# A four-stage transformer block on one core: moving transfers, landing rooms and waits in the second attention

## The chip, the core and the metric

The kernel runs on one core of a Trainium2 chip. The metric is the device time of one launch in microseconds (us). Engines are named as in the profile: PE is TensorE (matmuls), DVE is VectorE, ACT is ScalarE, POOL is GpSimd, and SP is SyncE, which issues most of the DMAs. "SPq" and "POOLq" are the issue queues of SP and POOL.

## The reference, cut to what matters

Four residual steps on `x` of 2 x 1024 rows by 512, all in float32:

```python
x = x + attn_a(layernorm(x))   # gated linear attention: 4 heads, chunks of 128 rows, carried state
x = x + ffn(layernorm(x))      # silu(gate) * up, then down; int32 weight codes, hidden size 1408
x = x + attn_b(layernorm(x))   # below
x = x + ffn(layernorm(x))      # the same weights again

def attn_b(x, W_q, W_k, W_v, W_o):
    Q, K, V = x @ W_q, x @ W_k, x @ W_v           # one head of 512
    attn = softmax(Q @ K.T / sqrt(512), axis=-1)  # 1024 x 1024 for each of 2 batches
    return (attn @ V) @ W_o
```

Most of the change lies in `attn_b`. It is computed with the weights folded beforehand (`wm` holds W_q times W_k transposed, `wvo` holds W_v times W_o), so that a tile of output is the probabilities times V', plus the residual row, divided by the sum of its row.

## The kernel before, in words

Rows are worked in 16 tiles of 128 (`NT` = 16, 8 for each batch). A float32 operand of PE is kept as a high and a low half: `split(hi, lo, src)` is a cast on ACT (`hi`, line 70) and a subtraction on DVE or POOL (`lo`, line 71); `mm3` (lines 84 to 86) multiplies with three matmuls, high by high, high by low and low by high. Each engine runs its instructions in the order in which the scheduler of the kernel's language has put them. `behind(...)` states that what follows is to stand behind given instructions; the lists `last`, `summed`, `ends` and `splits` hold such instructions. A DMA from SP is issued in that order too, and waits ahead of its issue for what it reads and for the room that it fills.

The stages, with their places in the span:

- The start: products of weights (`M` from W_q and W_k, `V` from W_v and W_o) are computed on PE, split and stored to DRAM by `spill` (line 168; two stores a block, high and low half). Layer norm of the first eight tiles goes through `ln_tile`, which ends in `layernorm`: statistics on DVE, the power -1/2 on POOL (`rs`, line 109), the scaling on DVE (`xn`, line 111), then a transpose on PE (`pxT`, line 119).
- Attention a: a loop over 16 tiles; `fill[t]` holds steps to be slipped in behind tile t. `a_split(2)` and `a_split(3)`, the splits of the normed rows of tiles 8 to 11 and 12 to 15, are in `fill[2]` and `fill[6]`. `kT` (line 601) is the copy of a tile's keys, needed by the scores `pS` (line 627).
- ffn f: two passes, with seven products where the block form has eight (`pX`, `pY`, `pZ`, `pV`, line 329). `stationary` (line 302) makes or loads the weights of one of 11 blocks; the first time, it casts int32 codes on ACT (`codes`) and keeps the result in DRAM (`wc`). Later passes load 896 KB for each block (`wcf`, `wcg`).
- Attention b: two batches b, each with four cycles n = 0 to 3. A cycle is written out as `scores_head` (four PSUM tiles, `psX`, `psV`, `psY`, `psZ`), something in between (`q_proj` or an `out_b`), `scores_tail`, and `softmax` of the tiles 2n and 2n+1: maxima `mx` and scaling `nm` on DVE, exponentials `pe` on ACT, row sums, `ri`.
- ffn g: like ffn f, from stored weights.

A tile's probabilities are turned so that PE can use them. `probs_T` transposes 32x32 blocks on DVE (`py`, line 1059), stores them to DRAM (`p<-py`, line 1063, 512 KB), and reads them back in four DMAs that place each block (`raw<-p`, line 1072, 128 KB each, in pieces of 32 floats). `raw` lands in a buffer with the tag `pe`, the room of the exponentials, of which there are two. `probs_split` casts it to `pth` and subtracts to `ptl`; `out_b` multiplies these with V' (24 matmuls into `pob`, lines 84 to 86) and adds the residual row `xrb`, loaded on POOL, on DVE (line 1097); line 1098 stores the result. Tile 14 is turned on PE (`ppt`) instead.

Between these steps the layer norm of ffn g goes on for the tiles that are done (`norm`: `ln_norm` for a tile, `ln_move` for a group of four tiles). `ln_move` turns a group by 16 small DMAs from SBUF to SBUF (`xT_g<-y_g`, line 199, 64 KB each, again in pieces of 32 floats). `moving` holds the steps of `combine`, which make ffn g's operands (`B_g`, `T_g`) from a turned group. `do(steps, n)` runs the next n of such a list behind the last softmax. The order of these calls is written out by hand in the loop over b that is printed below.

Of the kernel before, what the change touches and what calls it, by code (L numbers as in the profile page):

```python
# [16 lines left out]
P = 128  # L17
# [17 lines left out]
def hybrid_block_kernel(ctx: ExitStack, tc: tile.TileContext, a, out):  # L35
# [132 lines left out]
    def spill(pool, tags, ps, dst, name):  # L168
        for m in range(KD):
            hi, lo = (pool.tile([P, 512], F32R, tag=tags[m % len(tags)], name=f"{name}{m}_{j}") for j in range(2))  # L170
            done = split(hi, lo, ps[m])
            nc.sync.dma_start(out=dst[m][:, 0:512], in_=hi.bitcast(F32))
            nc.sync.dma_start(out=dst[m][:, 512:1024], in_=lo.bitcast(F32))
        return done

    lnT, lnY, lnX = {}, {}, {}
# [13 lines left out]
    def ln_move(nm, st, b):  # L190

        if b == 0:
            lnT[nm, st] = slot(f"xT_{nm}{st}").rearrange("p (k c) -> p k c", k=KD)
        y = lnY[nm, st]
        xf = lnT[nm, st].bitcast(F32).rearrange("p k (i b q) -> p (k i) b q", i=ST, b=4)
        for c in range(4):
            half = (nm, st) in (("b", 2), ("g", 0))
            sync = nm in "af" or (nm, st) in (("b", 0), ("b", 1), ("g", 3)) or (half and c % 2)
            (nc.sync if sync else nc.gpsimd).dma_start(
                out=xf[32 * b : 32 * (b + 1), :, c, :],  # L200
                in_=y[32 * c : 32 * (c + 1), b].rearrange("p k i q -> p (k i) q"),
            )
# [96 lines left out]

    saves = []  # L300

    def stationary(j, name, fresh=None, loaded=None, queue=None):


        w = slot(f"wc{name}_{j}").rearrange("p (n c) -> p n c", n=8)
        if fresh or loaded:
            a21, a11, s1, s2, s3, a12, s4, a22 = (w[:, n] for n in range(8))
            for n, (dst, nm) in enumerate(((w[:, 1:6:4], "cg"), (w[:, 0:8:7], "cu"))):
                room = (loaded[n], None) if loaded else fresh
                codes(*room, dst, a["wgu"][j][:, n * 512 : (n + 1) * 512], f"{nm}{name}_{j}")  # L310
            f = lambda x: x.bitcast(F32)
            nc.gpsimd.tensor_tensor(s1, f(a21), f(a22), ALU.add)
            nc.gpsimd.tensor_tensor(s2, f(s1), f(a11), ALU.subtract)
            nc.gpsimd.tensor_tensor(s3, f(a11), f(a21), ALU.subtract)
            nc.gpsimd.tensor_tensor(s4, f(a12), f(s2), ALU.subtract)
            saves.append(lambda: nc.sync.dma_start(out=wc_d[j], in_=f(w[:, 1:8])))
        else:
            (queue or nc.sync).dma_start(out=w[:, 1:8].bitcast(F32), in_=wc_d[j])
        return w

    def products(ps, w, nm, pr, n, first):
# [17 lines left out]
    with ExitStack() as actx:  # L339
# [354 lines left out]
        for i in range(4):  # L694
            ends.clear()
            q_head(0, i)
            with behind((wq_loaded, *ends.values())):
                for t in ((), (4,), (5,), (6, 7))[i]:
                    ln_tile(t)
            if i == 1:  # L700
                with behind((*normed_x, *copied)):
                    spill(ap, ("kT", "kw", "sdec", "at"), pm, m_d, "M")
# [17 lines left out]
                step()  # L720
            xTa[g] = lnT["a", g]

        fill[2].append(lambda: a_split(2))
        fill[6].append(lambda: a_split(3))
        moving = combine("f", 0)
        wcs, loads = [], []
        for t in range(NT):
            if t + 4 < NT:
                q_head(*divmod(t + 4, ST))
            if t == 0:  # L730
                decay_rows(0)
                load_row(0)
                load_row(1)
            load_row(t + 1)
            if t + 1 < NT:
                kv_tile(t + 1)
            weighed = scores(t)
            if t + 1 < NT:
                with behind((*(normed[t + 1][2:] or normed[t][2:]), *key_copy)):
                    decay(t + 1)  # L740
            if t == NT - 2:
                with behind(key_copy):
                    for n in (1, 2):
                        loads.append(product_operands(sp, a["WvT"], a["Wo"], "V", n))
                with behind(parts[-4:]):
                    late_norm.pop()()
            with behind(normed.get(t + 1, (weighed,))):
                for step in fill[t]:
                    step()
                if 1 <= t <= KH:  # L750
                    down_weights(sp, t - 1)
                for n in {NT - 3: (0,), NT - 1: (3,)}.get(t, ()):
                    loads.append(product_operands(sp, a["WvT"], a["Wo"], "V", n))
                if t == NT - 3:
                    first_codes = [
                        load_codes(xp, "xn", a["wgu"][0][:, n * 512 : (n + 1) * 512], f"cf0_{n}") for n in range(2)
                    ]
# [159 lines left out]
    with ExitStack() as bctx:  # L917
# [104 lines left out]
        def softmax(t, halves, casts=()):  # L1022
            mx = mp.tile([P, 2], F32, tag="mx", name=f"mx{t}")
            for s, x in enumerate(halves):
                nc.vector.tensor_reduce(mx[:, s : s + 1], x, AX.X, ALU.max)
            nm = mp.tile([P, 1], F32, tag="nm", name=f"nm{t}")
            nc.vector.tensor_scalar(nm, mx[:, 0:1], mx[:, 1:2], -SC, ALU.max, ALU.mult)
            pe = bp.tile([P, T], F32, tag="pe", name=f"pe{t}")
            rs = mp.tile([P, 2], F32, tag="rsum", name=f"rsum{t}")
            for s, x in enumerate(halves):  # L1030
                with behind(casts):
                    act = nc.scalar.activation(
                        pe[:, s * 512 : (s + 1) * 512], x, AF.Exp, bias=nm, scale=SC, accum_out=rs[:, s : s + 1]
                    )
            ri = mp.tile([P, 1], F32, tag="ri", name=f"ri{t}")
            nc.vector.tensor_tensor(ri, rs[:, 0:1], rs[:, 1:2], ALU.add)
            last[:] = act.ins, nc.vector.reciprocal(ri, ri).ins
            pes[t] = pe, ri

        def probs_T(b, i):  # L1040
# [24 lines left out]
            )  # L1065
            lo = bp.tile([P, NK, P], F32R, tag="ptl", name=f"ptl{t}")
            hi = bp.tile([P, NK, P], F32R, tag="pth", name=f"pth{t}")

            raw = bp.tile([P, T], F32, tag="pe", name=f"raw{t}").rearrange("p (k c) -> p k c", k=NK)
            placed = p_d[i].rearrange("k (c j) (r q) -> r j (k c) q", c=4, r=4)  # L1070
            for r in range(4):
                nc.sync.dma_start(  # L1072
                    out=raw[32 * r : 32 * (r + 1)].rearrange("p k (c q) -> p (k c) q", c=4), in_=placed[r]
                )
            ptT[t] = hi, lo, raw, ri

        def probs_split(b, i, after):
# [11 lines left out]
        def out_b(b, i):  # L1089
            t = b * NK + i  # L1090
            hi, lo, _, ri = ptT[t]
            xr = rp.tile([P, D], F32, tag="xres", name=f"xrb{t}")
            nc.gpsimd.dma_start(out=xr, in_=x2[t])
            po = psum(f"pob{t}")
            for k in range(NK):
                mm3(po, hi[:, k, :], lo[:, k, :], vs[b, k][0], vs[b, k][1], k == 0, k == NK - 1)
# [14 lines left out]
            vs[b, kt] = h_, l_  # L1111

        splits = []
        qs, QA, heads, pes, ptT, vs, last, summed = {}, {}, {}, {}, {}, {}, [], []

        def do(steps, n):
            with behind(last):
# [10 lines left out]
        def cycle(b, n, between):  # L1128

            array(scores_head, b, n)  # L1130
            if n > 0:
                for i in (2 * n - 2, 2 * n - 1):
                    if (b, i) != (1, 5):
                        probs_split(b, i, summed)
            if n in (0, 2):
                with behind(summed):
# [2 lines left out]
            if n == 1:  # L1139
                q_operands(b, 2, False)  # L1140
            array(scores_tail, b, n)
            if n < 3:
                with behind(last):
                    q_operands(b, n + 1, True)
# [3 lines left out]
        for b in range(NB):  # L1148
# [35 lines left out]
            for i in (0, 1):  # L1184
                probs_T(b, i)
            do(norm, 2)

            def between():
                q_proj(b, 1, (2, 3))
                if b:  # L1190
                    with behind(summed):
                        do(norm, 2)

            cycle(b, 1, between)
            for i in (2, 3):
# [100 lines left out]
```

## Time and profile before

| | |
|---|---|
| median of 3 runs | 958.59 us (958.22 to 959.99) |
| the profiled execution | 958.89 us, span 957.2 us |
| PE busy | 934.8 us, 98% of the span |
| DVE, ACT, POOL busy | 721.6, 412.4, 224.2 us |
| granted TensorE clock, mean | 0.995 |
| DMA | 162.18 MB in 218,805 packets, 155,056 of them under 512 bytes |

The span runs from the first to the last instruction of the profiled execution. Engines work side by side, so their busy times do not add up to it. The page of the profile also gives the span in 40 slices, with each engine's busy share and the clock that TensorE was granted, in tenths. Other views list what an engine waited for, the chain of waits that sets an end, and the sums of windows. Numbers at the end of a waits row are the total in us, the count and the longest; a landing time runs from a DMA's issue to its arrival.

The batch loop of attention b covers some 490 to 733 us. In its second batch, PE runs: scores of cycle 0 from 622.3, cycle 1 from 637.5, cycle 2 from 658.2, cycle 3 from 685.0; the last three `out_b` follow `ppt` at 706.

### The profile page before, as it was taken

To read this page: it belongs to the slowest core of one execution; us is meant where nothing else is said; L and a number is where in the kernel's file an instruction comes from. 1 tells how busy PE (TensorE), PEld (TensorE's weight loads), DVE (VectorE), ACT (ScalarE), POOL (GpSimd) and SP (SyncE) were. 2 spreads that over 40 slices of the span, in tenths; PEclk is the share of its full clock that TensorE was granted. 3 is DMA by queue.
4 is the path that set the end of the run, shared out by engine and by line. 5 is a ranking of instruction groups with operands and counts; after the bars stand their busy time and mean duration, and the time that the engine had idled before them with its cause. 6 is when DMAs were issued, how large, how long until landed. Compare 5 with 4: busy or idle time off the path is not lost.

```text
span 957.2 us, 13215 instructions
## 1 busy us (share of the span) xinstructions
PE 934.8 (98%) x4402; PEld 775.2 (81%) x4402; DVE 721.6 (75%) x1461; ACT 412.4 (43%) x795; POOL 224.2 (23%) x324
## 2 busy tenths in 40 slices
PE   9999999999999999999999999999896999999998
PEld 7788888898788878888888888888675888888887
DVE  7767767779899699769938778489675976976655
ACT  5554343345665344345234443244342443534421
POOL 3233323444553011111121302023200341001100
PEclk9999999999999999999999999999998999999999
DMA  9426456675898457724735879157987762463112
GB/s 326 171 100 176 133 122 170 195 184 195 295 331 292 116 189 260 205 45 149 267 69 95 170 154 245 64 97 150 160 173 229 271 190 45 177 239 145 39 60 84
DMA packets 218805, 162.18 MB, mean 169 GB/s; under 512 B 155056, under 2 KB 170736, under 8 KB 218736
## 3 DMA queue, kind: packets, MB, share of 16 engines
q1 hardware_dynamic: 215120, 151.10, 54.8%
q0 software_dynamic: 3616, 10.23, 5.0%
q8 instruction: 35, 0.57, 0.3%
q14 instruction: 34, 0.28, 0.1%
HBM read 104.76 MB, written 41.84 MB: 153 GB/s over the span
## 4 chain that ended last, share of the span: by engine, by line
PE 84%; DVE 5%; DMA 5%; SPq 3%; ACT 2%; issue 1%; POOL 0%; ACTq 0%
PE pog L889 4%; PE pog L888 4%; PE pVg L329 4%; PE pZg L329 4%; PE pXg L329 4%; PE pXf L329 4%; PE pZf L329 4%; PE pVf L329 4%; PE pof L889 3%; PE pof L888 3%; SPq L1072 3%; PE pYg L329 2%; PE pYf L329 2%; DMA raw<-p 2%; PE pob L84 2%; PE pob L85 2%
## 5 line engine op out<-in xcount | busy, mean ns | idle before, releaser
L84 PE MATMUL pob<-vh,pth 128*128 128x512 f32 x128 | 51.6, 403 | 12.0 <-ACT pth L70 12.0
L888 PE MATMUL pog<-wdg,hsg 128*128 128x512 f32 (+1 forms) x165 | 60.1, 375 | 0.0
L889 PE MATMUL pog<-wdg,hsg 128*128 128x512 f32 (+1 forms) x165 | 60.1, 375 | 0.0
L889 PE MATMUL pof<-wdf,hsf 128*128 128x512 f32 x154 | 59.1, 390 | 0.5 <-DVE hsf L71 0.5
L888 PE MATMUL pof<-wdf,hsf 128*128 128x512 f32 x154 | 58.9, 390 | 0.0
L85 PE MATMUL pob<-vl,pth 128*128 128x512 f32 x128 | 51.2, 400 | 0.0
L86 PE MATMUL pob<-vh,ptl 128*128 128x512 f32 x128 | 51.2, 400 | 0.0
L71 POOL TENSOR_TENSOR hsg<-sgg,hsg 128x128 fp32r<-128x128 f32 x40 | 18.0, 470 | 130.6 <-ACT hsg L70 130.6
L329 PE MATMUL pVf<-T_f,wcf 128*128 128x512 f32 x176 | 46.9, 390 | 1.2 <-ACT hbf L816 1.2
L329 PE MATMUL pXg<-B_g,wcg 128*128 128x512 f32 x176 | 46.6, 389 | 0.0
L329 PE MATMUL pVg<-T_g,wcg 128*128 128x512 f32 x176 | 46.3, 389 | 0.0
L329 PE MATMUL pXf<-B_f,wcf 128*128 128x512 f32 x176 | 45.4, 391 | 0.0
L109 POOL TENSOR_TENSOR rs_b<-ve_b,mhalf 128x1 f32<-128x1 f32 x16 | 13.1, 827 | 119.0 <-DVE ve_b L107 118.9
L70 ACT CAST pth<-raw 128x512 fp32r<-128x512 f32 x30 | 17.1, 619 | 55.0 <-DMA raw<-p 55.0
L329 PEld LDWEIGHTS pVf<-T_f,wcf 128*128 128x128 f32 x176 | 33.0, 188 | 8.5 <-ACT hbf L816 1.7
L84 PEld LDWEIGHTS pob<-vh,pth 128*128 128x128 f32 x128 | 24.8, 194 | 18.0 <-ACT pth L70 13.0
L71 DVE TENSOR_TENSOR ptl<-raw,pth 128x512 fp32r<-128x512 f32 x30 | 19.6, 688 | 26.0 <-ACT pth L70 25.9
L329 PEld LDWEIGHTS pXf<-B_f,wcf 128*128 128x128 f32 x176 | 32.9, 188 | 7.2 <-ACT hbf L816 0.4
L329 PEld LDWEIGHTS pXg<-B_g,wcg 128*128 128x128 f32 x176 | 33.0, 188 | 6.9
L329 PEld LDWEIGHTS pVg<-T_g,wcg 128*128 128x128 f32 x176 | 33.0, 188 | 6.9
L888 PEld LDWEIGHTS pog<-wdg,hsg 128*128 128x128 f32 x165 | 31.1, 188 | 5.7
L889 PEld LDWEIGHTS pog<-wdg,hsg 128*128 128x128 f32 x165 | 31.0, 188 | 5.6
(336 smaller groups left out, 2746.8 us busy)
## 6 DMA issues: line engine op xcount, KB each, us to landing
wcg<-wc SPq DMA_DIRECT2D x20, 896.0 KB, 5.3
wc<-wcf SPq DMA_DIRECT2D x11, 896.0 KB, 7.2
wcf<-wc SPq DMA_DIRECT2D x11, 896.0 KB, 5.1
p<-py SPq DMA_DIRECT2D x15, 512.0 KB, 3.8
raw<-p SPq DMA_DIRECT2D x60, 128.0 KB, 4.2
xin_a<-in_x SPq DMA_DIRECT2D x16, 256.0 KB, 5.1
xra<-in_x SPq DMA_DIRECT2D x16, 256.0 KB, 2.8
row<-cl SPq DMA_DIRECT2D x16, 256.0 KB, 3.8
```

Source lines behind the costliest of these rows:

```text
L70: c = nc.scalar.copy(hi, src)
L71: return c.ins, (eng or nc.vector).tensor_tensor(lo, src, hi.bitcast(F32), ALU.subtract).ins
L84: nc.tensor.matmul(ps, lhs_hi, rhs_hi, start=first, stop=False)
L85: nc.tensor.matmul(ps, lhs_hi, rhs_lo, start=False, stop=False)
L86: end = nc.tensor.matmul(ps, lhs_lo, rhs_hi, start=False, stop=last).ins
L109: nc.gpsimd.tensor_tensor(rs, ve, mhalf, ALU.pow)
L329: nc.tensor.matmul(ps, w[:, m, k * P : (k + 1) * P], o[:, s, k, :], start=first and k == 0 and s == 0, stop=k == 1 and s == 1, skip_group_ ...
L888: nc.tensor.matmul(ps, hs[i][0][:, j], wd[j][:, ds], start=j == 0, stop=False)
L889: nc.tensor.matmul(ps, hs[i][1][:, j], wd[j][:, ds], start=False, stop=j == KH - 1)
L1072: nc.sync.dma_start(out=raw[32 * r : 32 * (r + 1)].rearrange("p k (c q) -> p (k c) q", c=4), in_=placed[r])
```

## The change

1. In `probs_T`, `raw` is no longer a buffer of its own: the read lands in the room of the low half `ptl`, and the subtraction of the split works in place. Only tile 15 still uses a `pe` room.
2. In `out_b`, the residual row is loaded by SP, not POOL; for the last three tiles the load stands behind the last read of probabilities. The first two weight blocks of ffn g are loaded by SP too.
3. `ln_move` of group (g, 0) goes wholly on POOL (half of it was on SP). The norm steps of the second batch are given out in other cycles: two steps that stood between the scores of cycle 1 come after the cycle, and two steps of `moving` that stood ahead of cycle 2 come behind the scaling of its last softmax.
4. The split of tile (1, 3) goes behind the scaling `nm` of the last softmax of cycle 2.
5. `spill` stores the low halves of `V` on POOL.
6. `a_split(2)` and `a_split(3)` leave `fill` and go behind the copy of the key at t = 3 and t = 7.
7. `ln_tile` of tiles 5, 6 and 7 goes behind the scaling of the normed tile before (`normed_x`).

```diff
@@ spill
             nc.sync.dma_start(out=dst[m][:, 0:512], in_=hi.bitcast(F32))
-            nc.sync.dma_start(out=dst[m][:, 512:1024], in_=lo.bitcast(F32))
+            low = nc.gpsimd if name == "V" else nc.sync
+            low.dma_start(out=dst[m][:, 512:1024], in_=lo.bitcast(F32))
@@ ln_move
-            half = (nm, st) in (("b", 2), ("g", 0))
-            sync = nm in "af" or (nm, st) in (("b", 0), ("b", 1), ("g", 3)) or (half and c % 2)
+            sync = nm in "af" or (nm, st) in (("b", 0), ("b", 1), ("g", 3)) or ((nm, st) == ("b", 2) and c % 2)
@@ the start
-            with behind((wq_loaded, *ends.values())):
+            with behind((wq_loaded, *ends.values(), *(normed_x if i > 1 else ()))):
                 for t in ((), (4,), (5,), (6, 7))[i]:
                     ln_tile(t)
@@ attention a
-        fill[2].append(lambda: a_split(2))
-        fill[6].append(lambda: a_split(3))
...
+            if t in (3, 7):
+                with behind(key_copy):
+                    a_split(t // 4 + 2)
@@ softmax
-            nc.vector.tensor_scalar(nm, mx[:, 0:1], mx[:, 1:2], -SC, ALU.max, ALU.mult)
+            scaled[:] = [nc.vector.tensor_scalar(nm, mx[:, 0:1], mx[:, 1:2], -SC, ALU.max, ALU.mult).ins]
@@ probs_T
-            raw = bp.tile([P, T], F32, tag="pe", name=f"raw{t}").rearrange("p (k c) -> p k c", k=NK)
+            raw = lo.bitcast(F32)
+            if t == NT - 1:
+                raw = bp.tile([P, T], F32, tag="pe", name=f"raw{t}").rearrange("p (k c) -> p k c", k=NK)
...
-                nc.sync.dma_start(
-                    out=raw[32 * r : 32 * (r + 1)].rearrange("p k (c q) -> p (k c) q", c=4), in_=placed[r]
-                )
+                back[:] = [
+                    nc.sync.dma_start(
+                        out=raw[32 * r : 32 * (r + 1)].rearrange("p k (c q) -> p (k c) q", c=4), in_=placed[r]
+                    ).ins
+                ]
@@ out_b
-            nc.gpsimd.dma_start(out=xr, in_=x2[t])
+            with behind(back if t >= NT - 3 else ()):
+                nc.sync.dma_start(out=xr, in_=x2[t])
@@ cycle
-                    if (b, i) != (1, 5):
+                    if (b, i) not in ((1, 3), (1, 5)):
                         probs_split(b, i, summed)
...
             array(scores_tail, b, n)
+            if (b, n) == (1, 2):
+                probs_split(1, 3, scaled)
+                with behind(scaled):
+                    for _ in range(2):
+                        moving.pop(0)()
@@ the loop over b
-            def between():
-                q_proj(b, 1, (2, 3))
-                if b:
-                    with behind(summed):
-                        do(norm, 2)
-
-            cycle(b, 1, between)
+            cycle(b, 1, lambda: q_proj(b, 1, (2, 3)))
             for i in (2, 3):
                 probs_T(b, i)
-            do(norm, 4)
+            do(norm, 4 if b == 0 else 6)
             array(out_b, b, 0)
             if b:
                 moving = combine("g", 0)
-                do(moving, 2)
...
-        wcs = [stationary(n, "g0", queue=nc.gpsimd) for n in range(2)]
+        wcs = [stationary(n, "g0") for n in range(2)]
```

More of the change, by code (lines that the diff above doesn't have):

```diff
@@ L300, in hybrid_block_kernel, with stationary @@
     saves = []
-    def stationary(j, name, fresh=None, loaded=None, queue=None):
+    def stationary(j, name, fresh=None, loaded=None):
         w = slot(f"wc{name}_{j}").rearrange("p (n c) -> p n c", n=8)
@@ L317, in stationary @@
         else:
-            (queue or nc.sync).dma_start(out=w[:, 1:8].bitcast(F32), in_=wc_d[j])
+            nc.sync.dma_start(out=w[:, 1:8].bitcast(F32), in_=wc_d[j])
         return w
@@ L1113, in hybrid_block_kernel @@
         splits = []
-        qs, QA, heads, pes, ptT, vs, last, summed = {}, {}, {}, {}, {}, {}, [], []
+        qs, QA, heads, pes, ptT, vs, last, summed, back, scaled = {}, {}, {}, {}, {}, {}, [], [], [], []
         def do(steps, n):
```

## The prediction

> **What bounds the kernel now.** I read the page first. TensorE (PE) is busy for 934.8 of 957.2 us, so the kernel is a stream of matmuls and an edit gains only where that stream stands still. The row of clocks has one slice at 8 where the others have 9, and the busy row has an 8 beside it: something is wrong near three quarters of the span.
>
> ```profile
> PE 934.8 (98%) x4402; PEld 775.2 (81%) x4402; DVE 721.6 (75%) x1461; ACT 412.4 (43%) x795; POOL 224.2 (23%) x324
> PE   9999999999999999999999999999896999999998
> PEclk9999999999999999999999999999998999999999
> ```
>
> Then what PE waited for (total, times, longest). The first line is nearly all of it: two waits of `out_b` (PSUM tile pob) for the cast of the probabilities (pth), 12.0 us together.
>
> ```profile
> PE pob L84 <- ACT pth L70: 12.0, 2, 7.8
> PE pxT_a L119 <- DVE xn_a L111: 1.4, 2, 1.0
> PE pVf L329 <- ACT hbf L816: 1.2, 1, 1.2
> PE pS L627 <- ACT kT L601: 1.2, 2, 0.7
> ```
>
> Windows around the two waits (PE busy, DVE, ACT, POOL, clock, DMA share, GB/s) show that each also costs clock afterwards.
>
> ```profile
> 674.60:678.00 3.40, 0.25 (x1) 0.25 (x2) 0.27 (x1) 0.92 (x2) 1.95 (x4) 1.00 1.31 149
> 678.00:681.40 3.40, 3.40 (x9) 2.39 (x9) 3.40 (x8) 1.23 (x4) 0.00 (x0) 0.50 1.42 142
> 722.40:725.80 3.40, 0.00 (x1) 0.01 (x1) 0.02 (x1) 0.67 (x2) 0.00 (x0) 0.50 1.06 255
> 725.80:729.20 3.40, 3.40 (x8) 2.68 (x9) 1.27 (x2) 0.47 (x1) 0.00 (x0) 0.50 0.84 311
> ```
>
> In a half-clock window PE gets through about half (9 and 8 matmuls against 16 or 17 in the windows after), so some 1.75 us is lost each time: by PE's rows the 24 matmuls of out_b(1,2) run from 677.75 to 685.1 and those of out_b(1,7) from 725.8 to 733.1, 7.3 us each, against 5.44 (24 x 0.2267) at full speed. PE's rows leave 4.3 us idle before the first (to 677.75) and 8.0 before the second (to 725.8); 12.0 of these 12.3 is the wait listed. The tail of the second attention so loses 4.3 + 8.0 + 2 x 1.75 = **15.8 us**. That is the cap of any gain there.
>
> Why it waits is in the chain of waits over that stretch (start, us, what).
>
> ```profile
> 665.01 0.32 SPq L1072
> ...
> 677.13 6.49 DMA raw<-p
> 683.72 0.63 ACT pth L70
> ...
> 709.01 1.15 DVE py L1059
> 710.20 3.50 DMA p<-py
> 713.83 0.32 SPq L1072
> 714.20 1.50 SPq L1072
> 715.75 6.13 SPq L1072
> 721.92 3.11 DMA raw<-p
> 725.13 0.63 ACT pth L70
> ```
>
> First stall: the reads `raw<-p` of tiles 10 and 11 are issued from 665.0 to 679.5 and land late. Second: tile 15's exponentials (ACT rows at 707.3 to 708.8) come late, because the cycle before them was late, and then its four reads take 8.65 us to issue beside two 896 KB loads of wcg from POOL. Issue times of eight reads, alone and then in the first stall:
>
> ```profile
> L1072 SPq DMA_DIRECT2D raw<-p x8: 324/828/1826, 643.5 to 649.1; - x8
> DMA to landing us min/median/max: 3.5/4.3/4.6
> L1072 SPq DMA_DIRECT2D raw<-p x8: 318/1948/2562, 665.0 to 677.1; - x8
> DMA to landing us min/median/max: 6.1/7.6/8.7
> ```
>
> **A rule against the change.** What differs at 665 is POOL's 16 moves `xT_g<-y_g` (64 KB each, from 665.2 to 677.3), also in 128-byte pieces. The Trainium skill, "DMA: Bandwidth & Descriptors", section "Why small descriptors are slow (HBM only)", says that transfers between two places in SBUF are spared the penalty of small pieces. By it the moves are no great load, shifting them buys nothing, and the first stall stays (4.3 + 1.75 = 6.05 us less gain). The rows speak otherwise: eight reads are 8,192 pieces (1 MB by 128 bytes) and alone take 9.8 us from first issue to last landing; with the moves' 8,192 beside them it is 18.7 us, the same rate per piece. I follow the rows.
>
> **The change part by part**, on the profiled execution (958.89 us: span 957.2 and 1.69 around it; it stands 0.3 above the median 958.59).
>
> (1) *Reads land in the room of the low half (ptl).* The same 60 reads; no instruction is added. The exponentials' room (pe) comes free at the transpose py, so the next exponentials no longer wait for a cast. In exchange the read of tile t waits for the last matmul of out_b(t-2), and SP's stores and rows stand behind it. On PE about 15 us lie between the end of out_b(t-2) and the start of out_b(t) in batch 1 (669.4 to 685: scores 4.3, out_b 5.4, scores 5.7). First issue to cast takes 6.35 us alone (643.47 to 649.82) and 7.35 with neighbours. The narrowest place is tile 5 of batch 0: out_b(0,3) ends at 563.8, the data is needed at 573.4, so 9.6 us for 7.35: slack 2.
>
> (2) *Norms of g's tiles 6 and 7, and g's moves, come later.* All 16 moves then start behind the read of tile 10, at about 673. Tile 10: read from 665.4 alone, cast about 671.8, needed at 673.5. Tile 11: issued after out_b(1,1), lands about 675.7, needed much later. The first stall and its slow window go; I leave +0.3. Group (g,0)'s moves all go to POOL (8 more at about 0.65 us each, 627 to 638, where POOL is otherwise idle and PE has scores): 0.
>
> (3) *Scaling before splits.* nm of tiles 12 and 13 no longer queues behind the casts of tile 11. With (1), their exponentials come at 678.4 to 681 instead of 686 to 688.6. Downstream, PE itself sets the pace: cycle 3 starts near 680, tile 13's read goes out when out_b(1,3) ends (690.1) and lands at 696.5, casts to 697.9, tile 15's exponentials to 699.3, py 700.7, store 3.7 (landed 704.4), reads 3.7 to issue and 3 to land, cast at 710.8 to 711.2. PE needs it at 711.7 (out_b(1,4) ends 699.9, then two ppt and two out_b). Stall between 0 and 1.2, taken +0.7. The 8.0 and its slow windows go otherwise.
>
> (4) *Rows (16 x 256 KB) and the first wcg go from POOL to SP.* SP waits for the store three tiles back before it issues a row, about 2 us each (its waits of 2.9 and 2.1 us for x<-xrb in that stretch); cover: a row is issued one or two tiles ahead of its use. The last three rows and wcg stand behind tile 15's reads: issued 708 to 709.2. DVE's add for tile 13 then waits until about 712 and holds the second half of tile 15's low part, which out_b(1,7) reaches only 2.7 us after its start: covered. wcg_0 lands 5.3 (median) to 9.3 us (beside the reads) later, at 714.5 to 718.5, needed at 717.2: +0 to +1.3, taken +0.3.
>
> (5) *V's low stores on POOL.* Four stores of 256 KB leave SP, whose next load (codes) starts 2.8 us earlier. The scheduler puts codes of wcf_3 ahead of the cast hbf_0 on ACT, which frees the PSUM that pVf waits for. PE loses 2.4 to 2.85 us at 253 and 259 (pVf 1.2, pYf 0.9). With an earlier load I expect 0.5 to be left: -1.9; bounds -2.5 and +1.5 (hbf_0 behind two code casts of 0.73 us).
>
> (6) *The splits of a's groups 2 and 3 go behind the copy of the key.* ACT no longer does four casts (2.18 us at 88.31) ahead of kT: 1.2 us of waits go, and the first product of the new group waits about 0.45: -0.8.
>
> (7) *The last norms of attention a go behind normed_x.* Tile 4's xn comes earlier, so the wait of 1.0 at 29.4 goes. But rs of tiles 6 and 7 now stands behind two Wv subtractions on POOL (1.3 us each, to 36.4), and their xn behind ten instructions of DVE. Summing DVE's rows, they end at about 39.4 and 40.0; PE needs them from 36.1. pWv starts at 40.6 in place of 38.17: **+2.3**, bounds +1.5 and +2.9.
>
> *The clock there.* The Trainium skill, "TensorE: Matmul & The Clock Gate", "What's actually happening", halves the rate after an idle window of about 3.4 us. The first window above held 0.25 us of work and still brought 0.50. So by the rule a stop of 3.4 us must fill a window exactly and the sum gets +0; by the row a slightly longer reach will do, about one chance in five of +1.75. The likeliest case leaves it out; it is in the range.
>
> Sum: -15.8 + 0.3 + 0.7 + 0.3 - 1.9 - 0.8 + 2.3 = -14.9, so 958.9 becomes **944.0 us**. A difference under 0.2% (1.9 us) could not be told from no change here.
>
> **The rivals.**
> - *A second stall stays (0.14).* Tile 15's store waits on SP behind a row (2 to 3 us each), or its read shares the queues with moves or rows: cast 3 to 5 us late, a slow window, wcg behind it. For it: two of its links (store 3.5, reads 6.13 + 3.11) sit at fixed cost, with only 0.5 us to spare. Against: the wcg loads are now behind it. 944 + 3 to 8 = 947 to 952.
> - *The first stall only moves (0.10).* The move burst meets tile 11's or 13's read instead, or tile 5's: 12.1 us from issue to cast (665.0 to 677.1) against 9.6 is 2.5, and 1.75 of clock, in one or two places: 948 to 952.
> - *Slower (0.12).* SP's in-order queue becomes the bound: a read that waits two tiles back holds the next store, row and x3 store, and DVE's in-order add then stands on the row ahead of the next maxima, so every cycle pays. Place: cycles 2 and 3 of both batches, tile by tile. It decides once a read, from release to cast, takes more than 15 us, some 2 us beyond the collided read plus a row wait (12.1 + 2): six tiles at 1.5 to 2 us with 1.75 of clock each are 19 to 22 us, against 14.9 gained: 963 to 966. Against it: alone, a read takes half that.
> - *It does not do what it says (0.02):* the order of PE's instructions in the second attention is unchanged, and SP's and POOL's lists show each move, so hardly.
>
> **How the numbers follow.** Likeliest case 0.62: 941 to 947. Low end: -15.8 - 2.5 - 1.3 + 1.5 = -18.1, which is 941. The range runs to 953 to take in both middle rivals; outside lie the slower case and a little below. Faster 0.62 + 0.14 + 0.10 = 0.86, same 0.02, slower 0.12.
>
> **What would show it.** The 12.0 of pob for pth gone or under 1.5; all clocks at 9; the eight reads of tiles 10 and 11 near 0.9 us each; pxT_a's wait up from 1.4 to about 3.5; pS for kT gone; the first pXg at 717 to 718 (before 733.0). Wrong, if pob still waits over 3 us, if ppt or psX starts to wait, or if SP stands on pob for over 3 us with a store behind it.

## The result, and the profile after

The changed kernel takes 956.74 us (median of 13 runs, 955.05 to 958.57) where the kernel before takes 958.76 (13 runs, 958.11 to 959.99). The ratio is 0.9979 with a 95% interval of 0.997 to 0.9987: 2.0 us faster, where 14.9 were forecast. The profiled execution of the changed kernel took 955.05 us with a span of 953.3; it is the fastest of the 13, so its span lies 3.9 below that of before while the medians lie 2.0 apart.

From the page (busy time, the 40 slices, the clock) and the view of what PE waited for (total, times, longest):

```profile
PE 936.1 (98%) x4402; PEld 776.3 (81%) x4402; DVE 723.0 (76%) x1461; ACT 412.1 (43%) x795; POOL 220.5 (23%) x318
PE   9899999999899999999999999999999999999998
PEclk9999999999999999999999999999999999999999
...
PE pXf L329 <- ACT u2f L843: 4.7, 1, 4.7
PE pxT_a L119 <- DVE xn_a L111: 3.9, 1, 3.9
PE pob L84 <- ACT pth L70: 2.1, 1, 2.1
```

The 8 near three quarters of the span has gone, and with it 9.9 of the 12.0 us of `pob` for `pth`. Two waits that were not there have come in elsewhere: 4.7 us in ffn f, and 3.9 at the start, where 1.4 stood. The second slice (from 24 us) and the eleventh (from 238 us) now show an 8. Windows around the three stops (length, then busy time of PE, PEld, DVE, ACT and POOL, clock, DMA share, GB/s):

```profile
36.40:39.80 3.40, 0.00 (x0) 0.00 (x0) 3.40 (x10) 1.96 (x4) 2.35 (x3) 0.96 0.83 265
39.90:43.30 3.40, 3.40 (x13) 3.07 (x14) 2.20 (x6) 1.97 (x3) 0.00 (x0) 0.56 0.50 154
257.30:260.70 3.40, 0.00 (x0) 0.00 (x0) 0.00 (x0) 1.65 (x3) 0.13 (x1) 1.00 0.98 338
261.40:264.80 3.40, 3.40 (x10) 2.62 (x9) 1.98 (x4) 0.26 (x2) 2.00 (x3) 0.50 1.03 392
701.60:705.00 3.40, 1.26 (x6) 0.70 (x5) 0.16 (x1) 0.81 (x2) 0.00 (x0) 1.00 1.22 159
705.10:708.50 3.40, 3.40 (x9) 2.39 (x9) 2.48 (x6) 1.18 (x4) 0.00 (x0) 0.50 0.68 116
```

Each stop is followed by a window at half clock, so each costs more than its wait. The mean clock of these two executions hides this (0.995 in both): three half-clock windows were there before (one at 678, two from 722) and three are there after, but at other places. Between executions it shows. The fastest of the 13 of the changed kernel had a mean clock of 0.995, the slowest (958.57 us) 0.991: some two windows more, by the estimate that one takes half of 3.4 us out of 955.

Setting the start of the same PE instruction in one trace against the other gives the account by stage (after minus before): +4.0 us by `pcum` (before at 41.0), back to +2.7 by 143 us after the copies of the key (-1.3), +7.4 in ffn f at 267 us (+4.7), +8.4 when attention b has run to 650 us, and -3.6 at the first `pXg` (729.42, before 732.98). The last step is the tail of attention b: -12.0.

The reads that the change was to spare look as the prediction wanted. For tiles 10 and 11 (before: issues of 1948 ns in the median, landings of 7.6 us) and for tile 15 (before: 8.65 us for the four issues), by the tiles `ptl` and `raw` of the changed kernel:

```profile
L1076 SPq DMA_DIRECT2D ptl<-p x8: 302/560/1491, 674.4 to 680.4; - x8
DMA to landing us min/median/max: 3.0/4.0/5.1
```
```profile
L1076 SPq DMA_DIRECT2D raw<-p x4: 318/619/731, 716.8 to 718.5; - x4
DMA to landing us min/median/max: 3.0/3.8/4.2
```

`out_b(1,2)` starts at 681.86 without a wait. What is left of `pob` for `pth` is in `out_b(1,4)`, and the chain of waits of the changed kernel tells what makes it late (start, us, what):

```profile
689.43 1.15 DVE py L1060
690.58 0.03 DVE ri L1037
690.61 7.12 DMA p<-py
...
697.78 0.33 SPq L1076
...
700.31 3.79 DMA ptl<-p
...
704.19 0.63 ACT pth L70
704.82 0.04 issue
704.86 0.61 PE pob L84
```

The store of tile 12's probabilities takes 7.12 us where a store takes 3.8 in the median. The sixteen moves `xT_g<-y_g` of group (g,1) are issued from 682.63 to 693.6, and the store goes out in the midst of them.

### The profile page after: what moved, and what is told of

Its sections match the earlier page's. It is cut to its first block, busy times and chain, and to the rows that moved or that the text cites. A ratio compares the mean times of both kernels' runs of the same rounds, so it can differ in the third digit from the quotient of the medians.

```text
span 953.3 us, 13233 instructions
## 1 busy us (share of the span) xinstructions
PE 936.1 (98%) x4402; PEld 776.3 (81%) x4402; DVE 723.0 (76%) x1461; ACT 412.1 (43%) x795; POOL 220.5 (23%) x318
## 4 chain that ended last, share of the span: by engine, by line
PE 87%; DVE 5%; DMA 4%; SPq 2%; issue 1%; ACT 0%; POOL 0%; DVEq 0%; ACTq 0%; POOLq 0%
PE pog L890 4%; PE pog L889 4%; PE pVg L329 4%; PE pZg L329 4%; PE pXg L329 4%; PE pZf L329 4%; PE pVf L329 4%; PE pXf L329 4%; PE pof L890 3%; PE pof L889 3%; PE pob L84 3%; PE pob L86 3%; PE pob L85 3%; PE pYg L329 2%; PE pYf L329 2%; PE psV L988 2%
## 5 line engine op out<-in xcount | busy, mean ns | idle before, releaser
L109 POOL TENSOR_TENSOR rs_g<-ve_g,mhalf 128x1 f32<-128x1 f32 x16 | 9.6, 605 | 134.9 <-DVE ve_g L107 134.8
L199 POOL DMA_DIRECT2D xT_g<-y_g x48 | 30.9, 652 | 41.2 <-DVE T_b L71 29.8
L890 PEld LDWEIGHTS pof<-wdf,hsf 128*128 128x128 f32 x154 | 28.9, 188 | 8.1 <-DVE hsf L71 2.1
```

Source lines behind the costliest of these rows:

```text
L109: nc.gpsimd.tensor_tensor(rs, ve, mhalf, ALU.pow)
L199: (nc.sync if sync else nc.gpsimd).dma_start(out=xf[32 * b : 32 * (b + 1), :, c, :], in_=y[32 * c : 32 * (c + 1), b].rearrange("p k i q -> ...
L890: nc.tensor.matmul(ps, hs[i][1][:, j], wd[j][:, ds], start=False, stop=j == KH - 1)
```

## The experiments

All were run in five rounds beside the kernel before, which took 959.41 us in the first four, 959.23 in the next four and 959.18 in the last three. The theory after the result: (a) four V stores moved to POOL cost some 5 us, by the order of casts on ACT; (b) the late norms at the start cost some 5, stop and half-clock window together; (c) in the tail the moves' DMA work now meets a store. The rivals: the two new stops are shifts that the tail would give back anyway; POOL's issue queue, the landing room or the place of the store binds in the tail and not DMA work. Five of the kernels below carry a "hold": the first products of ffn g are put behind the last matmuls of `out_b`, so that PE keeps its order; by itself it changes no engine's order. But in the four of them whose rows stay on SP (moves on two queues, a room of their own, the old cycles, large pieces) the scheduler made another list for DVE at the end of attention b: the subtraction of tile 15 stands behind `B_g` and the add of a row, where it stood ahead of `B_g` and in part ahead of the add. All four lose 6 to 8 us between the end of `out_b(1,6)` and the first `pXg` (6.1 against the changed kernel; 6.2, 8.1 and 7.3 against the version with both early parts undone), whatever their edit. So their totals do not give the worth of their edits alone.

### V's low stores back on SP (change 5 undone)

```diff
-            low = nc.gpsimd if name == "V" else nc.sync
+            low = nc.sync
```

> The changed kernel with V's low stores back on SP, nothing else. Theory: in the changed kernel the scheduler put the two code casts of weight block 3 on ACT ahead of the copy u2f_2 and of hbf_0, the codes land at 258, and PE stands 4.7 us for u2f at 256 and then runs a half-clock window. With the stores on SP the order is that of before, so the wait for u2f goes, a wait of about 1.2 for hbf comes back, and the time falls by 4.7 to 6 us against the changed kernel, to about 951 to 952. Rival: the wait comes from the changed traffic around attention a (key copy, late norms), not from the stores' queue: then the wait stays and the time stays at 956 to 957.

Measured: 951.86 us, ratio 0.9929 (0.9916 to 0.9941), 4.9 below the changed kernel. What PE waited for:

```profile
PE pxT_a L119 <- DVE xn_a L111: 4.5, 2, 3.9
PE pob L84 <- ACT pth L70: 2.4, 1, 2.4
...
PE pVf L329 <- ACT hbf L817: 1.2, 1, 1.2
PE pYf L329 <- POOL wcf L313: 0.9, 1, 0.9
```

The wait for `u2f` has gone, and the small ones of before (1.2 and 0.9) are back. Why it had come is on ACT. In the changed kernel's timeline of ACT (start, us, instruction, what it was idle for) the two casts of codes stand ahead of `u2f` and `hbf`, and wait 4.86 us for their load:

```profile
258.28 0.72 ACT L293 ACTIVATE wcf<-cgf,zero 128x512 fp32r<-128x512 int32 x1 [4.86 <-DMA cgf<-in_wgu]
259.77 0.72 ACT L293 ACTIVATE wcf<-cuf,zero 128x512 fp32r<-128x512 int32 x1 [0.77 <-DMA cuf<-in_wgu]
260.40 0.57 ACT L843 COPY u2f<-pXf 128x512 f32<-128x512 f32 x1
260.87 0.69 ACT L817 ACTIVATE hbf<-pZf,cols 128x512 f32<-128x512 f32 x1
```

In the kernel before, one `hbf` and `u2f` came first (254.08 and 254.67) and the casts behind them (256.51 and 257.18). With the stores back on SP the old order is back, so it was their move that gave the casts an earlier place; that the scheduler counted on a shorter list of SP is inferred. But the load is no earlier: from the first V store's issue to the start of the first cast of codes it is 10.7 us before, 11.1 in the changed kernel, 11.3 here. SP took 4.76 us to issue its four stores, where it had taken 4.9 for eight; the other four were issued from POOL at the same time (from 247.33, in 2.40 us).

### The last norms of attention a as before (change 7 undone)

```diff
-            with behind((wq_loaded, *ends.values(), *(normed_x if i > 1 else ()))):
+            with behind((wq_loaded, *ends.values())):
```

> The changed kernel with the last norms of the start placed as before (not behind normed_x). Theory: the wait of pxT_a for xn_a of 3.9 us and the half-clock window behind it come from this alone; both go, the small wait of 1.0 at 29.4 comes back, and the time falls by about 4.0, to 952 to 953. Rival: the stop is set by the Wv subtractions on POOL and DVE themselves and would fall on the next consumer (pWv): then the time falls by under 1.5.

Measured: 951.31 us, ratio 0.9923 (0.9911 to 0.9936), 5.4 below the changed kernel. `pxT_a` for `xn_a` is down from 3.9 to 1.0 us, and there is no half-clock window at 40. The trace shows 3.9 of it by `pcum`. It can't show the rest: it is of the slowest of the five executions (954.23 us) and gives 3.0 of the 3.9 back further on, with two half-clock windows behind the wait for `u2f`, where the changed kernel's trace has one, and with three waits for `pth` (4.1 us) in place of one.

### Half of group (g,1)'s moves on SP

```diff
-            sync = nm in "af" or (nm, st) in (("b", 0), ("b", 1), ("g", 3)) or ((nm, st) == ("b", 2) and c % 2)
+            sync = nm in "af" or (nm, st) in (("b", 0), ("b", 1), ("g", 3)) or ((nm, st) in (("b", 2), ("g", 1)) and c % 2)
```

with the hold.

> The changed kernel with half of the 16 moves of ffn g's second group on SP and half on POOL (plus a placement that keeps PE's order at the end of the second attention as it is). Theory: the stores p<-py of tiles 12 and 13 (690.6, 7.1 us to land) are slow because POOL is still issuing moves until 693.6; with two queues the burst is over about 2 to 4 us earlier, the store lands in about 4, tile 12's cast comes by 701 to 702, the 2.1 us wait and its half-clock window go, and the time falls by up to 3.9, to about 953. Rival: the store and the reads are slow for what else is out (rows, stores of x3, SP's waits for lanes): SP has eight more DMAs now, so tile 12's cast comes no earlier or later, and the time stays or rises by 1 to 3.

Measured: 962.53 us, ratio 1.0032 (1.0019 to 1.0044), slower than both. From the timeline of SP in this kernel:

```profile
684.62 8.47 SPq L199 DMA_DIRECT2D xT_g<-y_g  x8 
...
694.80 1.36 SPq L1065 DMA_DIRECT2D p<-py  x2
```

SP needs 8.47 us for its eight moves, while POOL issues its eight from 684.59 in 5.17. The burst is issued in 8.5 us where POOL alone took 11.0, but the store that it was to clear the way for now stands behind it in SP's order and goes out at 694.80, to land in 4.55 us. Tile 12 gained by it: its wait is 1.3 us in place of 2.1, the half-clock window behind it is gone, and by the end of `out_b(1,6)` this kernel has won 2.2 us on the changed one since 700 us. It loses 6.1 behind that, where `out_b(1,7)` waits 2.1 us for `pth` and 2.0 for `ptl`, with DVE's other list. So the total does not say that POOL's issue rate was not what bound; the theory's gain of up to 3.9 came in part, and was lost elsewhere.

### The casts of codes behind u2f and hbf

V's stores stay on POOL; for the block that had moved ahead, the casts are stated to follow the two instructions of ACT.

```diff
+            with behind((freed, gated[0])):
+                wcs.append(stationary(3, ...))
```

> The changed kernel with V's low stores still on POOL, but the code casts of weight block 3 told to stand behind u2f_2 and hbf_0, as they stood before. It parts the queue from the order. Theory (order): the wait for u2f goes as in the run with the stores on SP, and the time falls by 4 to 6 us, to about 951 to 953. Rival (traffic): the eight stores and the codes share the same DMA engines wherever they are issued, PE then waits for the codes themselves a little later, and less than 2 us are won.

Measured: 957.04 us, ratio 0.9973 (0.9963 to 0.9984): no gain on the changed kernel. The wait for `u2f` has gone from PE's list, and this stands in its place:

```profile
PE pxT_a L119 <- DVE xn_a L111: 4.4, 2, 3.9
PE pZf L329 <- DVE pZf L852: 4.2, 1, 4.2
PE pob L84 <- ACT pth L70: 3.1, 2, 1.9
...
PE pXf L329 <- DMA wcf<-wc: 1.4, 1, 1.4
```

On DVE the addition into `pZf` starts at 264.92, behind two `hbf` and the `hsf` between them; before, it started at 259.81, ahead of `hsf` and of the second `hbf`. So repairing ACT's list alone hands the stop on to DVE; that DVE's list, too, was planned on the early load is inferred. That the order on ACT held PE is shown by the wait that went; that it can be mended at that place alone is refuted.

### Both undone (changes 5 and 7)

> The changed kernel with both early parts undone: V's low stores on SP and the last norms of the start as before. Theory: the two losses are independent of each other and of the second attention, so the time is that of the changed kernel less both: 956.7 - 4.9 - 5.4, about 946.5 (945.5 to 948). What is then left against before is the second attention's gain alone plus about 1.3 of the key copy. Rival: one of them only hides the other (the stall of ffn f's start depends on where the start leaves the queues): then 949 to 951.

Measured: **947.01 us**, ratio 0.988 (0.9861 to 0.9899). It beats both kernels, by 9.7 and 12.2 us, and is the best of all versions run. What PE waited for:

```profile
PE pxT_a L119 <- DVE xn_a L111: 1.8, 2, 1.0
PE pob L84 <- ACT pth L70: 1.8, 1, 1.8
PE pVf L329 <- ACT hbf L817: 1.5, 1, 1.5
```

The two edits are worth 4.9 + 5.4 = 10.3 one by one and 9.7 together (4.3 and 4.9, if the other is undone first): they add up, and nothing further on takes the gain away. The following versions start from this one.

### The store ahead of ffn g's operands

The store of tile 12 is to come earlier: the two `moving` steps go behind `py` of tile 12, and a norm step goes back between the scores of cycle 1.

```diff
-                with behind(scaled):
-                    for _ in range(2):
-                        moving.pop(0)()
...
+            if b:
+                do(moving, 2)
```

> As the run with both early parts undone, and in the second attention the transpose py of tile 12 ahead of the making of B_g on DVE, and tile 6's norm between the scores of cycle 1 again (so that the moves start some 2 us earlier). Theory: tile 12's wait (2.1 us, with its half-clock window) is a store that meets the last third of the moves; the store goes out about 2 us earlier and the moves end about 2 us earlier, the store lands about 4 us earlier, the wait goes: 3 to 4 us less than with both early parts undone, about 943. Rival: the store, now earlier, only overlaps more of the moves, lands as late as before, and the time stays at 946 to 947.

Measured: 948.04 us, ratio 0.9888 (0.987 to 0.9905), not to be told from 947.01. The store goes out at 678.99 in place of 682.83 and lands at 685.7 in place of 689.8, but then its reads take 9.04 us to issue and the cast starts at 695.11 in place of 695.75. What was won on the store went into the reads, as if the work in the window bound and not the store's place in it.

### The reads land in a room of their own (change 1 undone)

```diff
-            raw = lo.bitcast(F32)
-            if t == NT - 1:
-                raw = bp.tile([P, T], F32, tag="pe", name=f"raw{t}").rearrange("p (k c) -> p k c", k=NK)
+            raw = bp.tile([P, T], F32, tag="pe", name=f"raw{t}").rearrange("p (k c) -> p k c", k=NK)
```

with the hold.

> As the run with both early parts undone, with the reads of all tiles landing in a pe room again (as before), all else of the change kept. Theory: the moves' place is what takes the first stall away; the room matters less, since the reads of tiles 10 and 11 now land early and free pe in time: within 2 us of the run with both early parts undone. Rival (the prediction): without the room the exponentials of tiles 12 and 13 wait for the casts of tiles 10 and 11, tile 15 is late again, and 5 us or more of the gain are lost: 951 to 955.

Measured: 953.67 us, ratio 0.9946 (0.9932 to 0.9959), 6.7 above the version that it starts from. PE waits 3.4 us in two places for `pth` and 2.8 for `ptl`. Up to the end of `out_b(1,6)` this version is no later than the one that it starts from (0.3 us); all of the loss lies in `out_b(1,7)`. There the second half of tile 15's exponentials starts at 704.25 in place of 701.47. The subtraction of tile 13, which here reads one of the two `pe` rooms, ends at 704.21, just ahead of it; that fits the room as the cause. So the room matters, as the prediction had said and the theory by then no longer did. But the 2.8 for `ptl` are of DVE's other list; how much of the 6.7 is the room's was not separated.

### The norms and the moves in the old cycles (change 3 undone in part)

`between()` with its two norm steps is back, and `do(norm, 4)` after cycle 1; so the moves come earlier (from 667.59, where they started at 674.86). With the hold.

> As the run with both early parts undone, with the norms of ffn g's tiles 6 and 7 between the scores of cycle 1 again, so that the 16 moves start about 10 us earlier, beside the stores and reads of tiles 10 and 11. Theory: the moves collide with tile 10's read as before, the wait of out_b(1,2) comes back with 2 to 4 us and a half-clock window: 949 to 952. Rival: with the reads in ptl's room tile 10's read is out before the moves and the collision falls on tile 11's, which has 9 us to spare: then 943 to 947, better than the placement of the change.

Measured: 956.46 us, ratio 0.9968 (0.9957 to 0.9979), 9.4 above. Waits of 4.5 us for `pth` in three places, 2.5 for `ptl`, 1.6 for `pe`. The wait at tile 10, which the theory put at 2 to 4 us with a half-clock window, is 1.1 without one. The waits for `ptl`, for `pe` and one for `pth` of 2.5 lie at the last three tiles, with DVE's other list. So what the later moves of change 3 carry of the tail's gain is not shown.

### The moves in large pieces

The sixteen moves of group (g,1) write rows of 2 KB in place of pieces of 32 floats: the same bytes, the same number of issues, far fewer pieces. The kernel leaves out the placing of the turned blocks, so ffn g gets operands in the wrong order; it serves the timing alone.

```diff
+                out=lnT[nm, st]...rearrange("p k c -> p (k c)")[32 * b : 32 * (b + 1), 512 * c : 512 * (c + 1)]
```

with the hold.

> As the run with both early parts undone, but the 16 moves of ffn g's second group keep their number, bytes and places in the queues and write 2 KB rows where they wrote pieces of 128 bytes: they leave out the placing of the turned blocks. Theory: the number of pieces is what loads the DMA engines from 675 to 688; with a sixteenth of them the stores of tiles 12 and 13 land in about 4 us in place of 7, the cast of tile 12 comes 3 us earlier, its wait of 1.8 and the half-clock window go, and the time falls by 3 to 4 us, to 943 to 944. Rival: what delays the store is the number of DMAs in flight or POOL's own issue (0.65 us each): then the store still takes 7 us and the time stays at 947.

Measured: 949.77 us, ratio 0.99 (0.9883 to 0.9917). The timeline of SP, first with both undone, then with large pieces:

```profile
682.83 1.56 SPq L1064 DMA_DIRECT2D p<-py  x2
689.89 6.12 SPq L1076 DMA_DIRECT2D ptl<-p  x8
```
```profile
681.25 1.56 SPq L1069 DMA_DIRECT2D p<-py  x2
685.07 6.42 SPq L1081 DMA_DIRECT2D ptl<-p  x8
```

From the store's issue to the first read it is 7.06 us with small pieces and 3.82 with large ones. Tile 12's cast starts at 690.99 in place of 695.75, and `out_b(1,4)` at 692.81 without a wait. POOL also issues large pieces faster (its sixteen moves in 8.6 us, not 10.3), so fewer are still to come when the store goes out. But the moves load the DMA engines less, too. The POOL queue of the DMA table (packets, MB, share of 16 engines' span), in the same order:

```profile
q0 software_dynamic: 2304, 4.72, 3.4%
q0 software_dynamic: 2304, 4.72, 3.1%
```

So it is the small pieces of the moves that stretch the store, by the load of the pieces and by POOL's slower issue; the two were not parted. By the end of `out_b(1,6)` this kernel has gained 3.6 us on the version that it starts from, counted from 700 us. The whole did not gain by it: in DVE's other list the second half of tile 15 stood behind the add of another row, and PE waited 2.4 us for `ptl` and 1.4 for `pth`, with two half-clock windows. The mechanism is shown, and what it is worth up to there; a gain of the whole is not.

### The splits of a as before (change 6 undone)

`a_split(2)` and `a_split(3)` are in `fill[2]` and `fill[6]` again.

> As the run with both early parts undone, with the splits of groups 2 and 3 of attention a in their old place (ahead of the key copy). Theory: two waits of pS for kT, 0.7 and 0.55, come back and nothing else: +1.2 to +1.4, about 948.3. Rival: their new place also costs something elsewhere in attention a, so the time is the same or falls.

Measured: 947.45 us, ratio 0.9875 (0.9858 to 0.9892), 0.4 above and not to be told from 947.01. The waits of `pS` for `kT` are back (1.1 us). This version differs from the kernel before by the edits to attention b alone: they are worth 959.18 - 947.45 = 11.7 us, the same as the trace's 12.0.

### Rows and the first operands back on POOL (change 2 undone)

```diff
-                nc.sync.dma_start(out=xr, in_=x2[t])
+                nc.gpsimd.dma_start(out=xr, in_=x2[t])
...
-        wcs = [stationary(n, "g0") for n in range(2)]
+        wcs = [stationary(n, "g0", queue=nc.gpsimd) for n in range(2)]
```

with the hold.

> As the run with both early parts undone, with the residual rows and the first two weight blocks of ffn g on POOL again. Theory: the rows are worked far enough ahead that their queue doesn't matter in batch 0 and in most of batch 1; POOL then holds rows between the moves and the moves start or end later by up to 2 us, and two 896 KB loads run beside tile 15's reads again (8.65 us in before against 2.6): tile 15 comes 2 to 5 us late: 949 to 952. Rival: tile 15's reads have enough time now, and the time stays within 1 us of 947.

Measured: 956.41 us, ratio 0.9956 (0.9937 to 0.9975), 9.4 above by the medians. The twelve executions spread from 950.99 to 960.14 us, four of them under 952, and the trace is of the slowest. What PE waited for in it, first line:

```profile
PE pob L84 <- ACT pth L70: 10.9, 2, 5.9
```

That is near the 12.0 of before, but at tiles 12 and 15, not 10 and 15. In this kernel tile 15's reads take 7.2 us to land in the median (3.9 with both undone), for the two loads of `wcg` are on the way again. The stores of tiles 12 and 13 land in 8.08 and 11.70 us (7.01 and 8.28 with both undone). In the four faster executions some 4 to 5 us are lost in place of 9; there is no trace of one of them.

## Why the prediction was wrong, point by point

Numbers in brackets are the prediction's parts: (1) is change 1 of the list above, (2) is change 3, (3) is change 4, (4) is change 2; (5) to (7) are the changes of these numbers.

**What bounds the kernel: right.** PE's stops and the half-clock windows after them are where the time between the kernels went. The rows that the prediction set against the rule on small pieces read rightly too: moves between two places in SBUF in 8,192 pieces hold up a store, and with pieces of 2 KB at the same bytes they don't (7.06 us against 3.82).

**Account by part**, by medians of the experiments where there is one:

| step | predicted | measured | from |
|---|---|---|---|
| tail of attention b (1 to 4) | -14.5 | -11.7 | 947.45 against 959.18 |
| V's stores (5) | -1.9 | +4.9 | 956.74 - 951.86 |
| splits behind the key (6) | -0.8 | -0.4, within noise | 947.01 - 947.45 |
| late norms (7), with the clock | +2.3 | +5.4 | 956.74 - 951.31 |
| sum | -14.9 | -1.8 | measured whole: -2.0 |

**(5) is the step that failed, by 6.8 us, and in sign.** It went wrong at "with an earlier load". The issue of the load was to come 2.8 us earlier since four stores left SP; it came 4.8 us behind the first store where it had been 4.9, and the codes were there no earlier (11.1 us behind the first store where it had been 10.7). That the scheduler moved the casts ahead on ACT had been seen in its list; the bound of +1.5 took two casts of 0.73 and nothing for their wait on the load, which was 4.86. The Trainium skill, "DMA: Bandwidth & Descriptors", section "Issuing engines are not separate DMA queues", states that DMAs from different engines end up on the same 16 DMA engines, and that several issuers spare only the time of issue. By it the load could gain at most the time of issue; SP's 4.76 us for four stores against 4.9 for eight says that here not even that was spared.

**(7): the stop near right, the clock wrong.** PE restarts 2.7 us later than before (39.89 against 37.16), against 2.3 predicted and a bound of 2.9. The half-clock window behind it was given one chance in five and left out. It came in all four traces of a kernel with this stop: the changed one and the experiments with V on SP, with moves on two queues and with casts behind `u2f`. It began at 39.5, 40.2, 42.3 and 39.8 us there, so the stop does not fall at the same place of the windows each time. Its length is enough: a stop of 3.9 us over windows of 3.41 leaves one of them at most 1.45 us of work wherever it falls (an estimate, 3.41 less half of 3.93), and windows with up to 1.48 always brought half clock in these traces (last section). The Trainium skill, "TensorE: Matmul & The Clock Gate", "What's actually happening", asks for an idle window of about 3.4 us; the window 36.4 to 39.8 holds 0.00 of PE, but with moves on two queues the one ahead of half clock (38.88 to 42.29) held 1.16. The likeliest case should have held the window.

**The tail (1 to 4): right in its causes, 2.8 too good in its sum.** The stall of tile 10 went, and so did that of tile 15: term +0.3 held. The term that failed is +0.7, all of the residue at the four tiles 12 to 15. The working followed tile 13's and 15's read from store to cast at 3.7 us for a store, and never asked what else was on the queues when tile 12's store goes out. The moves, put at about 673 in the times of before, did start near there (682.63, less the 8.4 us by which this stage is late: 674.2), and run on for 11 us, over the store. Tile 12's cast so ends at 704.8, 2.1 us late, and a window at half clock follows, some 1.75 more. It is what the rival "the first stall only moves" describes, onto a store and not onto a read.

**(4) was costed at +0.3 and is worth -9.4 by the medians, -4 to -5 in the faster executions,** though the whole of the tail came out near: with rows and `wcg` back on POOL much of the gain of the rest goes. The prediction had listed the two loads as part of tile 15's stall and counted the gain there once, under (3). So the sum was not hurt, but a reader of its parts would have kept (3) and dropped (4).

**The rivals.** Slower by SP's order did not come in the change itself. With eight moves added to SP the kernel was slower (962.53), but it lost in `out_b(1,7)`, with DVE's other list, and not at the store that stood behind the moves; so that run does not speak for this rival. None of the cases had two stops outside attention b, and in the likeliest case each of the three terms outside it stood at one value.

**The signs given.** `pob` for `pth` under 1.5: no, 2.1. All clocks at 9: the slices show it, the windows don't. Reads of tiles 10 and 11 near 0.9 us each: 0.56 in the median. `pxT_a` near 3.5: 3.9. `pS` for `kT` gone: yes. First `pXg` at 717 to 718: 729.42; with both undone 721.11.

## What to carry to other kernels

Moving stores to another engine's queue need not bring the load behind them forward: here it landed no earlier, while the scheduler put work that waits for that load ahead of work that was ready, and mending one engine's list handed the stop to another. Before a stop is priced, ask whether it may fill a clock window, and what other DMA is on the way at every store and read that is on the path, not only at those that were late before. When a large gain and small edits come in one change, run it without each small edit: here two of seven edits ate ten of twelve microseconds. And before a run without one edit is read, compare where in the trace it loses: four runs here lost most at one place, under a new list of another engine.

## What the runs showed of the hardware

**A window need not be idle to bring half clock.** Window sums of the version with both undone:

```profile
693.90:697.30 3.40, 1.59 (x7) 0.69 (x6) 0.90 (x2) 1.14 (x2) 0.00 (x0) 1.00 1.18 156
697.30:700.70 3.40, 3.40 (x9) 2.66 (x10) 1.95 (x6) 1.60 (x5) 0.00 (x0) 0.50 0.57 106
```

PE was busy for 1.59 of 3.40 us, with a single wait of 1.8 us, and the next window ran at half clock. In the version with the late norms undone nearly the same work brought none:

```profile
699.79:703.20 3.41, 1.58 (x7) 0.94 (x5) 0.09 (x1) 0.47 (x1) 0.00 (x0) 1.00 1.12 160
703.20:706.61 3.41, 3.20 (x13) 2.36 (x14) 2.74 (x6) 1.19 (x3) 0.00 (x0) 1.00 1.01 147
```

The granted clock changes in steps of 3.41 us, at other places in each execution. Taken on these steps over all thirteen traces, half clock followed every window at full clock with up to 1.48 us of PE work and none from 1.74 on; around 1.6 it followed two (1.60 and 1.61) and not the third (1.58). So in these traces the limit lies near half of a window. Waits of up to 2.2 us in the version with the store first brought none: the windows around them held 2.2 us of work and more. By these limits a lone stop under some 1.7 us brings no half clock (3.41 less 1.74), one of 3.9 always does (twice 3.41 less 1.48), and between them its place in the windows decides; these two bounds are estimates. A stop of 1.8 us can so cost twice that. One idle window, as the section on the clock cited above has it, is too strict for these rows.

**An issue took longer with other DMAs on the way.** With moves on two queues, SP's eight moves of 64 KB took 0.59 to 1.55 us each to issue (8.47 in all), beside POOL's eight of 0.65 to 0.68 (5.17). SP took 4.76 us for four V stores beside four from POOL, where eight took 4.9 before.
